# Input transfers, TensorE's order and a few PSUM banks in a fused attention kernel

## The chip, the cores and the metric

The kernel runs on one core of one Trainium2 chip. A core has five engines with instruction queues of their own: TensorE (PE in the profile; PEld is its weight load), VectorE (DVE), ScalarE (ACT), GpSimd (POOL) and SyncE (SP), which here only issues DMAs. Engines meet through semaphores. The metric is device time in microseconds of one execution; lower is better. A page of the profiler and a trace of one profiled execution tell where the time goes.

## The reference, cut to what matters

Three stages, all float32. The input `x` has four samples of 128 channels and 64 x 64 positions (4096 tokens each).

```python
# layer 0: group norm, then attention over the positions of one sample, residual
e1 = prelu(w1 @ xn + b1)           # 64 x 4096, queries
e2 = prelu(w2 @ xn + b2)           # 64 x 4096, keys
asm = prelu(wa @ xn + ba)          # 128 x 4096, values
score = softmax(einsum('nci,ncj->nij', e1, e2), axis=2)
out = einsum('nij,ncj->nci', score, asm)
# layer 1: layer norm over channels, causal running softmax in 8 heads, residual
kv = silu(einsum('btd,ed->bte', x, W_kv)).reshape(b, t, 8, 128, 2)
s = einsum('hd,bthd->bth', q_proj, k)
m_A = cummax(s, axis=1); e = exp(s - m_A)
output = (cumsum(e[..., None] * v, axis=1) / cumsum(e, axis=1)[..., None]).mean(axis=2)
# ffn: 64 experts choose tokens by a gate; two dense layers with gelu; scattered back
```

Layer 0 carries most of the arithmetic: 4 x 4096 x 4096 scores and as many weights for the values.

## The kernel before, in words

**Layer 0.** A sample's queries are cut into 8 blocks (`NBLK`) of 512 (`BLK`), its keys into 16 steps of two chunks of 128. The main loop runs over (sample `b`, query block `qb`, step `p`). In each step `probs` (L563 to L575) has TensorE make two scores tiles (L567), has ACT take their exponential (L571) and DVE add it to an accumulator (L574); `weigh` (L582 to L594) has TensorE multiply the exponentials by the values into two PSUM banks (L592). The exponentials are made one step ahead: `probs(n + 1)` is recorded before `weigh(n)`.

**Preparation of a sample.** `preparation(b)` returns pieces that the loop records one at a time. The statistics are eight `bn_stats` over 512 columns each (L442), their aggregation (L445), and group means by two small matmuls against the constant matrix `gavg` (L449 to L461). Then for each block `k`: `normal(k)` (L468 to L474) writes `xn` on DVE, out of a pool of two buffers; `project(k)` (L488 to L516) multiplies it by the weights of queries and keys (L495), takes the bias on ACT into `y` (L501), forms the prelu (`prelu`, L476 to L486: `z`, the relu of `y`, and their sum `ee`), and sends `ee` to the buffers `e1` and `e2` by DMA; `value(k)` (L520 to L542) multiplies `xn` by the value weights in four matmuls (L525), adds the bias on DVE into `ya` (L537), and forms the prelu likewise into `am`. For sample 0 both write one PSUM tile of two banks, `whole`: projections bank 0, values bank 1.

**Sample 0** has nothing before it to hide its preparation. Its `x` comes in four transfers of 1024 columns, issued in turn by SP and ACT (`load_x`, L387 to L392), followed on ACT's queue by the small weights. `gavg` is built by POOL and DVE and scaled on DVE (L425). After the statistics the blocks 0 and 1 are projected (`work_off(own, 4)`, L661), then the loop starts. In each even step of the first block of queries two more pieces (`project(k)` and `value(k)`) are worked off, ahead of `probs(n + 1)` of that step (L669 to L673); that ends with block 7 in step 10.

**Who sets the order.** Outside a `manual_schedule` a scheduler orders each engine's instructions as it sees fit, subject to dependencies and to `tc.issue_after`, which puts an instruction behind a named one. Dependencies are tracked by tile. Inside a `manual_schedule` for PE, TensorE's instructions keep the order in which they are written. Before the change layer 0 was left to the scheduler, except for its last step, and layer 1's loop was under `manual_schedule`.

**Layer 1.** The loop (L1111 to L1185) runs over 32 blocks of 512 tokens. For block `n` it makes the keys of block `n + 1`: eight heads, each one matmul of 128x512 (L361) into a PSUM bank out of `ps_kv`, and one Silu on ACT (L362) that frees the bank (`keys`, L357 to L363). In the middle stand `weights` (L876 and on, transposes, ACT copy, masks), `values` (L916, Silu L920), the transposes of a later block's tokens (`turned`, L354), `totals` (L932, followed by additions into `before` on DVE, L942), `score`, `scan` (copies of scores, running maximum L834, subtraction L838, exponential L839, running sum, reciprocal; all but the exponential and two copies on DVE), `spread` (`rb`, the reciprocals spread through memory by DMA), and `outputs` (L952). The pools `ps_o` and `ps_t` have one buffer of two banks each: tile `o` is first written in `outputs(0)`, tile `t` in `totals(0)`. For `n = 0` all of block 1's keys come before `values(0)`; heads 4 to 7 of block 0 were made right before the loop's first scan.

**Tail.** After layer 1's loop come the gate and the experts, whose weights are loaded by DMA.

Of the kernel before, what the change touches and what calls it, by code (L numbers as in the profile page):

```python
# [8 lines left out]
F32 = mybir.dt.float32  # L9
AF = mybir.ActivationFunctionType  # L10
ALU = mybir.AluOpType
AX = mybir.AxisListType
PSUM = bass.MemoryType.PSUM
P = 128
# [4 lines left out]
def conv_attn_hybrid_kernel(  # L19
# [23 lines left out]
    nc = tc.nc  # L43
    B, C, N = x.shape
    R = w1t.shape[1]
    NH = qt.shape[1]
# [4 lines left out]
    BLK = 512  # L51
    NBLK = N // BLK
    CPB = BLK // P
# [26 lines left out]
    t = resid.tile([P, B * NCH, C], F32, tag="t", name="t")  # L80
# [245 lines left out]
    def open_banks(stack, pre=""):  # L326
        pool = opener(stack, pre)
        return pool("l1kv", 3, space=PSUM, side="right"), pool("l1s", space=PSUM, side="right")
# [25 lines left out]
            nc.tensor.transpose(ptr[:, c // 2, :, c % 2, :], xl, ident)  # L354
        return nc.scalar.copy(xt, ptr.rearrange("p q s u j -> p (q s u j)")).ins

    def keys(n, xt, heads, kss, ps, pre=""):  # L357

        for h in heads:
            pk = ps.tile([P, BLK], F32, tag="kv", name=f"{pre}pk_{n}_{h}")  # L360
            nc.tensor.matmul(pk, wks[:, h, :], xt, start=True, stop=True)  # L361
            nc.scalar.activation(kss[h], pk, AF.Silu)  # L362
        return [kss[h] for h in heads]  # L363
# [8 lines left out]
    with ExitStack() as l0:  # L372
# [13 lines left out]

        def load_x(b, queues):  # L387
            xs = one.tile([P, N], F32, tag="x", name=f"x_{b}")
            for q in range(4):
                cols = bass.ts(q, N // 4)  # L390
                queues[q % len(queues)].dma_start(out=xs[:, cols], in_=x[b, :, cols])
            return xs  # L392

        xs_of = {0: load_x(0, (nc.sync, nc.scalar))}
# [18 lines left out]
        bas = load("bas", [P, C], (every, ba.to_broadcast([P, C])))  # L413

        neg = wp.tile([P, 2], F32, tag="neg", name="neg")
# [6 lines left out]

        gavg = wp.tile([P, P], F32, tag="gavg", name="gavg")
        make_block_diagonal(nc, gavg, C // 32)
        nc.vector.tensor_scalar_mul(gavg, gavg, 32.0 / C)  # L425

        queries, keys_of, values_of, sent = {}, {}, {}, []

        def preparation(b):
# [34 lines left out]
            xn_of = {}  # L464

            whole = []

            def normal(k):  # L468
                xn = prep.tile([P, BLK], F32, tag="xn", name=f"xn_{b}_{k}")
# [6 lines left out]
            def prelu(dst, y, z, minus_a, negative):  # L476
                if negative is nc.vector:
                    nc.vector.tensor_scalar(
                        out=z, in0=y, scalar1=-1.0, scalar2=0.0, op0=ALU.mult, op1=ALU.max
                    )  # L480
                else:
                    nc.scalar.activation(z, y, AF.Relu, scale=-1.0)
                nc.scalar.activation(y, y, AF.Relu)
                nc.vector.scalar_tensor_tensor(
                    out=dst, in0=z, scalar=minus_a, in1=y, op0=ALU.mult, op1=ALU.add
                )  # L486

            def project(k):  # L488

                xn = xn_of[k]  # L490
                if b == 0:
                    if not whole:
                        whole.append(ps_x.tile([P, 2, BLK], F32, tag="x", name=f"whole_{b}"))
                    pe = whole[0]
                    nc.tensor.matmul(pe[:, 0, :], w12, xn, start=True, stop=True)  # L495
                else:
                    pe = ps_x.tile([P, 2, BLK], F32, tag="x", name=f"pe_{b}_{k}")
                    for u, h in enumerate(halves):
                        nc.tensor.matmul(pe[:, u, :], w12[h, :], xn[h, :], start=True, stop=True)
                y = prep.tile([P, BLK], F32, tag="y", name=f"y_{b}_{k}")  # L500
                nc.scalar.activation(y, pe[:, 0, :], AF.Identity, bias=b12)  # L501
                if b > 0:
                    nc.vector.tensor_add(y, y, pe[:, 1, :])
                z = prep.tile([P, BLK], F32, tag="z", name=f"z_{b}_{k}")
                ee = prep.tile([P, BLK], F32, tag="ee", name=f"ee_{b}_{k}")
                prelu(ee, y, z, neg[:, 0:1], nc.vector if (b, k) == (0, 0) else nc.scalar)
                e1 = qs_p.tile([P, BLK], F32, tag="e1", name=f"e1_{b}_{k}")
                queries[b, k] = e1

                queues = (nc.sync, nc.scalar) if (b, k) == (0, 0) else (nc.sync, nc.sync)  # L510
                by = ee.rearrange("r (j u p) -> r j u p", u=2, p=P)
                for u, (h, queue) in enumerate(zip(halves, queues)):
                    queue.dma_start(out=e1[h, :], in_=ee[halves[0], :])
                    moved = queue.dma_start(
                        out=e2[h, bass.ts(k, CPB // 2), :], in_=by[halves[1], :, u, :]
                    )  # L516
                if (b, k) != (0, 0):
                    sent.append(moved.ins)

            def value(k):  # L520
                xn = xn_of[k]
                if b == 0:
                    pa = whole[0].rearrange("p u (c d) -> p u c d", c=CPB)[:, 1:]
                    for c in range(CPB):
                        nc.tensor.matmul(  # L525
                            pa[:, 0, c, :], xn[:, bass.ts(c, P)], was, start=True, stop=True
                        )
                else:
                    pa = ps_x.tile([P, 2, CPB, C], F32, tag="x", name=f"pa_{b}_{k}")
                    for c in range(CPB):  # L530
                        for u, h in enumerate(halves):
                            nc.tensor.matmul(
                                pa[:, u, c, :], xn[h, bass.ts(c, P)], was[h, :],
                                start=True, stop=True,
                            )
                y = prep.tile([P, CPB, C], F32, tag="y", name=f"ya_{b}_{k}")
                nc.vector.tensor_tensor(  # L537
                    y, pa[:, 0], bas.unsqueeze(1).to_broadcast([P, CPB, C]), ALU.add
                )
                if b > 0:  # L540
                    nc.vector.tensor_add(y, y, pa[:, 1])
                z = prep.tile([P, CPB, C], F32, tag="z", name=f"za_{b}_{k}")  # L542
                prelu(am[:, bass.ts(k, CPB), :], y, z, neg[:, 1:2], nc.scalar)
# [9 lines left out]
        def work_off(blocks, n):  # L553
            for pre, f in blocks[:n]:
                pre()
                f()
            del blocks[:n]
# [24 lines left out]
        def weigh(b, qb, p, pr):  # L582
            am = values_of[b]
            if p == 0:
                av_of[b, qb] = [
                    ps_av.tile([P, BLK], F32, tag=f"av{u}", name=f"av_{b}_{qb}_{u}")
                    for u in range(2)
                ]
            for u in range(2):
                j = 2 * p + u  # L590
                for av, h in zip(av_of[b, qb], halves):
                    nc.tensor.matmul(  # L592
                        av, am[h, j, :], pr[h, u, :], start=(j == 0), stop=(j == NCH - 1)
                    )  # L594
# [63 lines left out]
        with tc.issue_after(root):  # L658
            nc.scalar.activation(seed[:, 1:2], eps5, AF.Exp)
        own = blocks  # L660
        work_off(own, 4)  # L661
        nxt = probs(*steps[0])
        first_sums(0, 0, nxt)
# [2 lines left out]
        end = l0.enter_context(ExitStack())  # L666
        for n, (b, qb, p) in enumerate(steps):
            pr = nxt
            if own and p % 2 == 0:  # L669
                work_off(own, 2)  # L670
                if not own:
                    with tc.issue_after(sent[-1]):
                        xs_of[1] = load_x(1, (nc.sync,))  # L673
            if n + 1 < len(steps):
                nxt = probs(*steps[n + 1])
            if n + 2 == len(steps):
# [3 lines left out]
                for i in range(2):  # L680
                    last_turned = turned(i, xls[i], xts[i], early_room[1])
            weigh(b, qb, p, pr)

            q0 = 1 if b == 0 else 0
            if (qb, p) == (q0, 0) and b + 1 < B:
# [12 lines left out]
            if (b, qb, p) == (B - 1, 1, 0):  # L698
                l0prep.close()
                early_room.append(open_room(early))  # L700
                xts, xl_place, kss = room_parts(early_room[0])
# [64 lines left out]
    def layer1(pre, ready):  # L766
# [6 lines left out]
        with ExitStack() as kept, ExitStack() as l1:  # L773
# [3 lines left out]
            xts, xl_place, kss = room_parts(room)  # L777
# [9 lines left out]
            if ready:  # L787
                ps_kv, ps_s = early_room[1:]
                l1.push(early_banks.pop_all())
            else:  # L790
                ps_kv, ps_s = open_banks(l1, pre)
            ps_o = pool("l1o", space=PSUM)
            ps_t = pool("l1t", space=PSUM)
# [7 lines left out]
            xt_of = {n: xts[n % 3] for n in range(NB)}  # L801
# [309 lines left out]
            def loop():  # L1111
                if ready:
                    ks = keys(0, xt_of[0], range(NH // 2, NH), kss, ps_kv)
# [6 lines left out]
                for n in range(NB):  # L1120
                    more = n + 1 < NB
                    if more:
                        ks = keys(n + 1, xt_of[n + 1], range(NH // 2), kss, ps_kv, pre)
# [4 lines left out]
                    if n + 2 < NB:  # L1128
                        xls = tokens(n + 2, xl_place)
                    if n == 0:  # L1130
                        ks += keys(n + 1, xt_of[n + 1], range(NH // 2, NH), kss, ps_kv, pre)
                    es, rr, _ = made
                    ems = weights(n, es)
                    if n >= 2:
# [126 lines left out]
            with tc.manual_schedule(engines={mybir.EngineType.PE}):  # L1261
# [130 lines left out]
                for g in range(EG):  # L1392
# [10 lines left out]
                    if ready:  # L1403
                        p, k = g // NBLK, g % NBLK
# [29 lines left out]
                for p in range(B // 2):  # L1434
# [8 lines left out]
                    for k0, OB in ((0, 1), (1, 1), (2, 2), (4, 2), (6, 1), (7, 1)):  # L1443
                        for k in range(k0, k0 + OB):
# [10 lines left out]
                            for z in range(2):  # L1455
                                n = (2 * p + z) * NBLK + k
                                at = t[:, bass.ts(n, CPB), :].rearrange("c i x -> c (i x)")
                                nc.vector.tensor_add(at, at, pss[z])
                        for z in range(2):
                            n = (2 * p + z) * NBLK + k0  # L1460
# [65 lines left out]
```

## Time and profile before

| what | us |
|---|---|
| median of 3 runs | 2394.99 |
| lowest to highest | 2394.41 to 2396.77 |
| the profiled execution | 2395.19 |
| its span | 2393.5 |
| start of the first projection (L495) | 14.39 |
| start of the second projection | 20.07 |
| one step of layer 0 in later blocks | 2.57 |
| last copy of the first block's result (L605) | 88.17 |
| first keys of layer 1 (L361) | 1463.73 |

The mean granted clock of TensorE is 0.996. Times in the trace are counted from the start of the span; the profiled execution's own time has 1.7 us more than its span. A line of the timeline gives the start, the duration of a run of like instructions, the engine, the line of code, the operation, output and inputs with their sizes, the number of instructions, and in brackets the idle time of that engine ahead of it with what ended the wait. One float32 matmul of the program shows as two records (x2).

The last transfers are another stretch of interest: in the last 94 us the DMA engines are busy 0.85 of the time and move 332 GB/s, while TensorE is busy 79 of the 94.

### The profile page before, as it was taken

The numbers are of one execution on the slowest core, as the hardware profiler recorded it, in microseconds if no ns is written. First come the engines' busy times: TensorE is split into PE (matmuls) and PEld (weight loads), VectorE is DVE, ScalarE is ACT, GpSimd is POOL, SyncE is SP. The second block draws the span as 40 slices with busy tenths as digits, with TensorE's granted clock in tenths as the row PEclk, the third lists the DMA queues.
The fourth block names the chain that finished last, engine by engine and source line by source line (L and its number), as shares of the span: only waits on it lengthen the run. The fifth ranks groups of instructions, "written<-read, shape, count | busy, mean of one in ns | idle before, by whom it ended". The sixth has DMA issues, their size and how long they took to land.

```text
span 2393.5 us, 45621 instructions
## 1 busy us (share of the span) xinstructions
PE 2347.4 (98%) x19416; PEld 1556.4 (65%) x19416; DVE 1493.6 (62%) x2594; ACT 1208.1 (50%) x1639; POOL 301.4 (13%) x337
## 2 busy tenths in 40 slices
PE   7999999999999999999999999999999999999887
PEld 3467767677778677778777775555555555655553
DVE  5666666666655666655555556666666677776655
ACT  5454444444443444444443435666666666666541
POOL 0000000000000000000000001343343433333300
PEclk9999999999999999999999999999999999999999
DMA  3200020001110000020000000212112121112388
GB/s 81 75 23 14 23 62 1 12 18 23 49 25 1 12 18 23 14 56 1 1 1 1 1 1 19 55 38 52 41 38 55 38 51 42 38 38 55 118 309 318
DMA packets 61189, 109.93 MB, mean 46 GB/s; under 512 B 10032, under 2 KB 35120, under 8 KB 60976
## 3 DMA queue, kind: packets, MB, share of 16 engines
q1 hardware_dynamic: 57536, 101.22, 14.7%
q10 hardware_dynamic: 3440, 5.70, 0.7%
q8 instruction: 154, 2.52, 0.4%
q14 instruction: 59, 0.48, 0.1%
HBM read 85.40 MB, written 8.91 MB: 39 GB/s over the span
## 4 chain that ended last, share of the span: by engine, by line


## 5 line engine op out<-in xcount | busy, mean ns | idle before, releaser
L592 PE MATMUL av<-pr,am 64*128 64x512 f32 x4096 | 1066.2, 591 | 0.0
L571 ACT ACTIVATE pr<-sc 128x1024 f32<-128x1024 f32 x512 | 523.2, 1022 | 676.5 <-PE sc L567 607.7
L574 DVE TENSOR_TENSOR acc<-acc,pr 128x1024 f32<-128x1024 f32 x480 | 586.7, 1222 | 440.4 <-ACT pr L571 440.3
L592 PEld LDWEIGHTS av<-pr,am 64*128 64x128 f32 x4096 | 637.8, 187 | 260.3 <-issue 46.8
L567 PE MATMUL sc<-e,e 64*128 64x512 f32 x2048 | 629.3, 593 | 0.0
L567 PEld LDWEIGHTS sc<-e,e 64*128 64x128 f32 x2048 | 320.2, 187 | 107.6 <-issue 24.5
L361 PE MATMUL pk<-room,wks 128*128 128x512 f32 x512 | 241.1, 610 | 2.6 <-ACT room L362 2.4
L916 PE MATMUL pv<-wvs,room 128*128 128x512 f32 x512 | 226.4, 595 | 2.3 <-ACT v L920 2.3
L920 ACT ACTIVATE v<-pv 128x512 f32<-128x512 f32 x256 | 152.5, 597 | 69.9 <-PE pv L916 69.9
L362 ACT ACTIVATE room<-pk 128x512 f32<-128x512 f32 x256 | 148.0, 597 | 56.7 <-PE pk L361 56.4
L916 PEld LDWEIGHTS pv<-wvs,room 128*128 128x128 f32 x512 | 97.0, 191 | 121.0 <-issue 113.3
L806 POOL MEMSET ew<- 128x1024 f32 x1 | 1.0, 951 | 1364.4 <-PE av L592 1364.4
L904 DVE TENSOR_TENSOR em<-em,rb 128x1024 f32<-128x1024 f32 x64 | 78.4, 1225 | 151.0 <-DMA rb<-rd 150.9
L361 PEld LDWEIGHTS pk<-room,wks 128*128 128x128 f32 x512 | 90.5, 190 | 109.4 <-issue 80.3
L895 POOL TENSOR_TENSOR em<-et,mask 128x1024 f32<-128x1024 f32 x64 | 122.6, 1935 | 82.2 <-ACT et L882 82.2
L952 PEld LDWEIGHTS po<-v,em 64*64 64x64 f32 x4096 | 113.1, 134 | 29.5 <-DVE before L942 26.7
L96 POOL TENSOR_SCALAR xg<-t,gmv,grs 128x128 f32<-128x128 f32 x120 | 94.8, 802 | 287.3 <-DVE grs L92 199.3
L952 PE MATMUL po<-v,em 64*64 64x128 f32 x4096 | 121.1, 273 | 2.5 <-issue 2.5
L854 DVE RECIPROCAL rr<-rr 128x512 f32<-128x512 f32 x32 | 107.3, 3353 | 1.1
L839 ACT ACT_TABLE_LOAD x24 | 30.8, 1283 | 119.8 <-DVE ss L838 119.8
L942 DVE TENSOR_TENSOR before<-before,pt 128x128 f32<-128x128 f32 x256 | 72.5, 283 | 9.6 <-PE pt L932 3.8
L849 DVE TENSOR_TENSOR_SCAN rr<-ones,state,ss 128x512 f32<-128x512 f32 x28 | 42.0, 1502 | 48.1 <-ACT ss L839 48.1
(199 smaller groups left out, 2025.7 us busy)
## 6 DMA issues: line engine op xcount, KB each, us to landing
rb<-rd SPq DMA_DIRECT2D x128, 256.0 KB
fw<-in_fw_dram SPq DMA_DIRECT2D x40, 512.0 KB
room<-in_fw_dram SPq DMA_DIRECT2D x18, 512.0 KB
t<-in_xtok_dram SPq DMA_DIRECT2D x32, 256.0 KB
e<-ee SPq DMA_DIRECT2D x63, 128.0 KB
x<-in_x_dram SPq DMA_DIRECT2D x14, 512.0 KB
e<-ee SPq DMA_DIRECT2D x63, 64.0 KB
out_dram<-t SPq DMA_DIRECT2D x8, 256.0 KB
```

Source lines behind the costliest of these rows:

```text
L96: i = engine.tensor_scalar(out=dst, in0=t[:, chunk, :], scalar1=mean, scalar2=rs, op0=ALU.subtract, op1=ALU.mult)
L361: nc.tensor.matmul(pk, wks[:, h, :], xt, start=True, stop=True)
L362: nc.scalar.activation(kss[h], pk, AF.Silu)
L567: nc.tensor.matmul(sc[:, u, :], e2[halves[u], p, :], e1[halves[u], :], start=True, stop=True)
L571: nc.scalar.activation(pr, sc, AF.Exp)
L574: added.append(nc.vector.tensor_add(acc, acc, pr).ins)
L592: nc.tensor.matmul(av, am[h, j, :], pr[h, u, :], start=(j == 0), stop=(j == NCH - 1))
L854: inverse = nc.vector.reciprocal(rr, rr).ins
L895: nc.gpsimd.tensor_tensor(em, eq.unsqueeze(2).to_broadcast([P, 2 * NH, H2]), mask.unsqueeze(1).to_broadcast([P, 2 * NH, H2]), ALU.mult,)
L916: nc.tensor.matmul(pv.rearrange("p h d -> p (h d)"), xt[:, bass.ts(2 * q + s, P)], wvs[:, bass.ts(m, BLK)], start=True, stop=True,)
L920: last = nc.scalar.activation(v[:, bass.ts(m, HPB), :], pv, AF.Silu).ins
L952: nc.tensor.matmul(po[s * H2 : (s + 1) * H2, u, q, :], aas[q][half, s, h, :], vs[2 * q + s][half, h, :], start=(q == 0 and h == 0), stop=F ...
```

## The change

1. Sample 0's `x` comes in eight transfers of 512 columns instead of four of 1024, on the same two queues in turn.
2. `gavg` is scaled on POOL instead of DVE.
3. The addition `ya` of sample 0's block 0 is put behind `ee` of the same block on DVE.
4. TensorE keeps the written order from the first projections to the end of the first block of queries, and the pieces of `own` blocks are worked off after `weigh` of the step, no longer before `probs`.
5. In layer 1's first round, heads 4 to 7 of block 1's keys are written to the two banks of tile `o` and the two of tile `t`, instead of banks of `ps_kv`.

```diff
-    def keys(n, xt, heads, kss, ps, pre=""):
+    def keys(n, xt, heads, kss, ps, pre="", banks=None):
 
         for h in heads:
-            pk = ps.tile([P, BLK], F32, tag="kv", name=f"{pre}pk_{n}_{h}")
+            if banks:
+                pk = banks.pop(0)
+            else:
+                pk = ps.tile([P, BLK], F32, tag="kv", name=f"{pre}pk_{n}_{h}")
             nc.tensor.matmul(pk, wks[:, h, :], xt, start=True, stop=True)
             nc.scalar.activation(kss[h], pk, AF.Silu)
...
-            for q in range(4):
-                cols = bass.ts(q, N // 4)
+            m = NBLK if b == 0 else 4
+            for q in range(m):
+                cols = bass.ts(q, N // m)
                 queues[q % len(queues)].dma_start(out=xs[:, cols], in_=x[b, :, cols])
...
-        nc.vector.tensor_scalar_mul(gavg, gavg, 32.0 / C)
+        nc.gpsimd.tensor_scalar_mul(gavg, gavg, 32.0 / C)
...
+            scaled = []
...
-                prelu(ee, y, z, neg[:, 0:1], nc.vector if (b, k) == (0, 0) else nc.scalar)
+                scaled.append(
+                    prelu(ee, y, z, neg[:, 0:1], nc.vector if (b, k) == (0, 0) else nc.scalar)
+                )
...
-                nc.vector.tensor_tensor(
-                    y, pa[:, 0], bas.unsqueeze(1).to_broadcast([P, CPB, C]), ALU.add
-                )
+                with ExitStack() as order:
+                    if (b, k) == (0, 0):
+                        order.enter_context(tc.issue_after(scaled[0]))
+                    nc.vector.tensor_tensor(
+                        y, pa[:, 0], bas.unsqueeze(1).to_broadcast([P, CPB, C]), ALU.add
+                    )
...
         own = blocks
+        written = ExitStack()
+        written.enter_context(tc.manual_schedule(engines={mybir.EngineType.PE}))
         work_off(own, 4)
...
-            if own and p % 2 == 0:
-                work_off(own, 2)
-                if not own:
-                    with tc.issue_after(sent[-1]):
-                        xs_of[1] = load_x(1, (nc.sync,))
+            if (b, qb, p) == (0, 1, 0):
+                written.close()
...
             weigh(b, qb, p, pr)
+            if own and p % 2 == 0:
+                work_off(own, 2)
+                if not own:
+                    with tc.issue_after(sent[-1]):
+                        xs_of[1] = load_x(1, (nc.sync,))
...
                     if n == 0:
-                        ks += keys(n + 1, xt_of[n + 1], range(NH // 2, NH), kss, ps_kv, pre)
+
+                        banks = []
+                        for ps, tag in ((ps_o, "o"), (ps_t, "t")):
+                            free = ps.tile([P, 2, BLK], F32, tag=tag, name=f"{pre}pk_{tag}")
+                            banks += [free[:, u, :] for u in range(2)]
+                        ks += keys(
+                            n + 1, xt_of[n + 1], range(NH // 2, NH), kss, ps_kv, pre, banks
+                        )
```

`prelu` now returns its last instruction, so that `scaled[0]` names it.

## Prediction before the run

> **What bounds the kernel now.** I read the page first: which engine is full, which lines fill it, whether it has gaps.
>
> ```profile
> PE 2347.4 (98%) x19416; PEld 1556.4 (65%) x19416; DVE 1493.6 (62%) x2594; ACT 1208.1 (50%) x1639; POOL 301.4 (13%) x337
> ...
> L592 PE MATMUL av<-pr,am 64*128 64x512 f32 x4096 | 1066.2, 591 | 0.0
> ...
> L361 PE MATMUL pk<-room,wks 128*128 128x512 f32 x512 | 241.1, 610 | 2.6 <-ACT room L362 2.4
> ```
>
> TensorE is busy 98% of the span; the chain of waits on the page is empty. Only what TensorE idles (2393.5 - 2347.4 = 46 us), or does more slowly than it could, can be won. What is lost anywhere before the closing stage stays lost to the end. So I took the timeline in three stretches, those that the change touches. The front, DVE and TensorE:
>
> ```profile
> 8.41 2.47 DVE L442 BATCH_NORM_STATS2 stats<-x 128x6 f32<-128x512 f32 x4 [0.15 <-DMA x<-in_x_dram]
> 10.80 0.21 DVE L425 TENSOR_SCALAR gavg<-gavg 128x128 f32<-128x128 f32 x1
> 10.92 0.37 DVE L445 BATCH_NORM_AGGREGATE mv<-stats 128x2 f32<-128x48 f32 x1
> ...
> 17.21 2.08 PE L525 MATMUL whole<-was,xn 128*128 128x128 f32 x8 [0.78 <-ACT y L501]
> ...
> 19.33 0.69 DVE L537 TENSOR_TENSOR ya<-whole,bas 128x512 f32<-128x512 f32 x1 [1.71 <-PE whole L525]
> 19.93 0.74 DVE L484 SCALAR_TENSOR_TENSOR ee<-z,neg,y 128x512 f32<-128x512 f32 x1
> 20.07 2.08 PE L495 MATMUL whole<-xn,w 128*128 128x512 f32 x2 [0.78 <-DVE ya L537]
> ```
>
> Reader: the last statistics, then `gavg`, then the aggregation run back to back; later the second projection waits for `ya`, the last reader of the one tile `whole`. The value matmuls wait for `y`, which reads the *other* bank of that tile: waits go by tile, not by bank. The first block of queries, one period (43.60 to 52.14, 8.54 us, two steps):
>
> ```profile
> 43.60 1.12 PE L495 MATMUL whole<-xn,w 128*128 128x512 f32 x2
> 44.65 1.12 PE L567 MATMUL sc<-e,e 64*128 64x512 f32 x2
> 45.70 1.16 PE L525 MATMUL whole<-was,xn 128*128 128x128 f32 x8
> 46.79 0.69 PE L567 MATMUL sc<-e,e 64*128 64x512 f32 x1
> ...
> 52.14 1.12 PE L495 MATMUL whole<-xn,w 128*128 128x512 f32 x2
> ```
>
> No idle, but half a score pair is drawn in between projection and value, alone, and the pair's other half comes later. The start of layer 1:
>
> ```profile
> 1468.37 1.28 ACT L362 ACT_TABLE_LOAD   x1
> 1469.66 1.57 ACT L362 ACTIVATE room<-pk 128x512 f32<-128x512 f32 x3
> 1470.31 4.22 PE L361 MATMUL pk<-room,wks 128*128 128x512 f32 x6 [2.02 <-ACT room L362]
> 1475.11 7.03 PE L916 MATMUL pv<-wvs,room 128*128 128x512 f32 x16
> ...
> 1491.01 3.74 PE L361 MATMUL pk<-room,wks 128*128 128x512 f32 x8
> 1492.97 1.57 ACT L362 ACTIVATE room<-pk 128x512 f32<-128x512 f32 x3
> ```
>
> TensorE stands 2.02 us for a bank while ACT loads tables; from 1471.6 to 1475.0 its granted clock is 0.50 (window 1472 to 1474), so six matmuls take 4.22.
>
> **What the Trainium skill says.** "TensorEngine Tiling (Array Packing)", Key Properties: a change of tiling mode drains TensorE. The trace agrees: projections of 128*128 among scores of 64*128 take 1.12 where two halves of 0.43 would do, about 0.2 a change. "TensorE: Matmul & The Clock Gate", Part 1: the clock is halved after a mostly idle window of about 3.4 us, on a free-running grid. Here the half-rate stretch is 3.41 long, after a window that was 0.41 busy; windows of 0.55 and more were not punished.
>
> **The change, part by part.**
>
> *Front.* The eight transfers end when four did: from 2 to 8 us the DMA share was 0.97 at 355 GB/s. But the last arrival is followed by two statistics (0.62 each) instead of four: 2 x 0.62 = 1.24 sooner; `gavg`, 0.13, goes to POOL, idle there. ACT issues two transfers more; its small loads now queue behind x, but its table load, ending 11.6, is needed only at about 12.0. `neg` now stands among the group sums and its `a` lands just in time. So normalisation starts 1.24 to 1.37 sooner. It is then given back: in the built order DVE has z, *xn of the third block*, `ee`, `ya`. That xn needs one of two xn buffers, freed by the first block's value matmuls, which end at 19.3 before, 18.05 after. Then 0.04 for the wait, 0.5 xn, 0.66 `ee`, 0.69 `ya` (each without its overlap): 19.95, against 20.02. In before, `ya` went first. The second projection starts 20.00 instead of 20.07: gain 0.07. The clock is half until 27.8 in either.
>
> *First block.* Now TensorE runs as written: scores(n+1), weigh(n), then projection and value with no work between. A period is two steps of 2.57 (5.14, from steady steps of later blocks), projection to end of `y` with the wait (1.16 + 0.69 + 0.06 = 1.91), value with its mode change 1.09: 8.14. Saved 0.40 a period: the split pair's 0.86 and two mode changes go, a wait for `y` of 0.75 comes, with nothing to cover it. Five periods: 2.0. At the start 0.43 is lost: scores twice (24.89 to 28.2, clock half until 27.8), weigh to 29.9, third projection there, fourth at 38.05, which is 35.48 with the extra step of 2.57 taken off; before 35.05. Sum -1.57, the front's 0.07 in it. Does anything come late? Behind the projection, ACT has y, z, relu, za, relu, exp: value ends 3.0, `ya` 3.74, za and relu (0.63 each) to 5.02, exp (1.02) to 6.04; its weigh is due at 3.0 + 0.86 + 1.71 + 0.86 = 6.43. Margin 0.39. e2's DMA has 2 us.
>
> *Layer 1, second block's keys.* Heads 4 to 7 now get two tiles of two banks each, which nobody reads yet. But the dependency is by tile: in the built program head 5 waits for the Silu of head 4, head 7 for that of head 6. Head 5 used to wait for head 2's Silu. ACT's Silus start at 1469.66 (table load) and take 0.52 each: heads 2, 3, 4 end 1471.23. So head 5 starts 1471.27 instead of 1470.31: +0.96. Head 7 waits for Silu 6: head 6's matmul 0.43 after head 5's, its Silu behind Silu 5, about 0.75 of idle: together **+1.7**. The half-rate window still follows, as the window before it is as idle.
>
> Second, DVE's order in that round changes: all six `before` additions (L942) and em stand ahead of the copies of the next scan. Before, three of these were between. About 0.28 each, with the hop to TensorE: the subtraction ends 8.77 after the second block's transposes instead of 7.66. Its Silus release the banks of keys(2), which in before came exactly in time (1493.57). **+1.1**.
>
> *Sum.* -1.57 + 1.7 + 1.1 = +1.2 on the profiled execution, 2395.19 (span 2393.5 and 1.7 around it): 2396.4. The median lies 0.2 below the profiled execution: **2396.2**. TensorE has no gap over 0.5 us between 1493 and 2246, and the last weights are loaded after the loop, so the shift arrives.
>
> Bounds of what the trace of before doesn't show: the two bank waits 0 to 1.7 (taken 1.7, as waits by tile are seen in `whole`); a second half-rate window, 0 to 1.7, as the 0.75 gap falls into it (taken 0); the DVE order 0 to 1.1 (taken 1.1); the front -1.2 to 0 (taken -0.07).
>
> **Rivals.**
>
> A. *The banks are free as meant.* Heads 4 to 7 run through, the window is kept busy, and the 2.02 wait and half clock go, 3.7. But the next scan then waits: rb of the first block lands at 1482.7 whatever TensorE does, em and the scan come behind it, and keys(2) stands about 2.8. Net -0.85. With -1.57: 2392.8, 2392.6 on the median's scale. For it: the banks were unused. Against: the built waits.
>
> B. *Slower: exp comes late in the first block.* Place: ACT, six periods. The margin is 0.39, over six hops between engines which I took at 0.04 to 0.06. From 0.39 on, each 0.1 costs 0.6. If one accumulation of 1.22 (L574) gets ahead of `ya` in time, each period loses 0.83: 6 x 0.83 = +5.0: 2401.2. For it: the chain through ACT and DVE is long and nothing covers it. Against: in the built order `ya` stands behind the accumulation that should be over by 0.53. It decides (over 0.2%) from a lateness of 1.0.
>
> C. *Everything as meant.* The front keeps 1.24, the first block 1.57, the keys 3.7: -6.5, 2388.7, 2388.5 on the median's scale. Against: each of the two givings-back above would have to be absent.
>
> D. *The order doesn't do what it says*: the built order shows it does; only its price is open.
>
> **How the numbers follow.** The likeliest 0.55, own range 2394.2 to 2398.4 (bank waits half as long, or a second half-rate window and more); A 0.12; B 0.22; C 0.11. About 0.2%, 4.8 us, is what a measurement of this kernel tells from no change: 2390.2 to 2399.8. The likeliest and A lie within: 0.67 same. B is slower, 0.22; C faster, 0.11. The range for 8 in 10 takes in the likeliest, A and most of B: 2391.0 to 2401.5.
>
> **What would show it.** Right: first projection near 13.1, but the second still at 20.0; periods of 8.14 with a wait for `y` of 0.7; block end 86.5; in the keys of block 1 two waits on ACT with heads 5 and 7, the first near 3.0; a wait of about 1 at keys(2). Wrong: the second projection at 18.8; periods of 8.5 and more, or a wait of weigh for exp (B); heads 4 to 7 with no wait (A).

## The result, and the profile after

| | before | after |
|---|---|---|
| median of 20 runs, us | 2396.32 | 2400.03 |
| lowest to highest | 2394.41 to 2398.76 | 2397.74 to 2403.41 |
| the profiled execution, us | 2395.19 | 2401.64 |
| its span | 2393.5 | 2399.9 |

The changed kernel takes 1.0015 times as long as the one before, 95% interval 1.0008 to 1.0022. That is 3.7 us slower, clear of noise but inside the 0.2% that the prediction called no change. (Ratios and intervals here and below are worked out from all runs, so they need not be the quotient of the medians beside them.) The two profiled executions are 6.4 us apart: before's was 1.1 under its median, after's 1.6 over. So the traces overstate the difference by 2.7; what in them is chance is named below.

The page's first line after:

```profile
PE 2346.9 (98%) x19416; PEld 1563.0 (65%) x19416; DVE 1494.8 (62%) x2593; ACT 1208.6 (50%) x1639; POOL 303.6 (13%) x338
```

TensorE's busy time is 0.5 us shorter than before, in a span that is 6.4 us longer. On the page the loss is idle time, but the page adds up stretches of opposite sign. From 14 to 95 us TensorE idles 8.2 us instead of 2.8, although the first block ends only 1.5 later, so its matmuls take less time in all. From 1463 to 1500 us it idles 4.6 instead of 2.0, and there more of its matmuls run at half clock. So each of the prediction's three stretches is read for itself. First the front of after, DVE and TensorE (columns as before: start, duration, engine, line, operation, count, and in brackets the wait):

```profile
7.64 2.72 DVE L446 BATCH_NORM_STATS2 stats<-x 128x6 f32<-128x512 f32 x4 [0.52 <-DMA x<-in_x_dram]
10.39 0.37 DVE L449 BATCH_NORM_AGGREGATE mv<-stats 128x2 f32<-128x48 f32 x1
...
18.86 0.55 DVE L475 TENSOR_SCALAR xn<-x,gst,std 128x512 f32<-128x512 f32 x1 [1.71 <-PE whole L532]
19.32 0.75 DVE L489 SCALAR_TENSOR_TENSOR ee<-z,neg,y 128x512 f32<-128x512 f32 x1
19.98 0.69 DVE L547 TENSOR_TENSOR ya<-whole,bas 128x512 f32<-128x512 f32 x1
...
20.72 2.07 PE L500 MATMUL whole<-xn,w 128*128 128x512 f32 x2 [1.90 <-DVE ya L547]
```

Aggregation starts at 10.39, 0.53 sooner than before's 10.92. Then `xn`, `ee` and `ya` stand in a row, and the second projection waits 1.90 for the last: it starts at 20.72, 0.65 *later* than before.

The first block of queries, TensorE alone:

```profile
39.68 1.12 PE L500 MATMUL whole<-xn,w 128*128 128x512 f32 x2
41.58 1.16 PE L532 MATMUL whole<-was,xn 128*128 128x128 f32 x8 [0.78 <-ACT y L506]
42.67 1.13 PE L577 MATMUL sc<-e,e 64*128 64x512 f32 x4
43.63 1.88 PE L602 MATMUL av<-pr,am 64*128 64x512 f32 x8
45.35 1.02 PE L577 MATMUL sc<-e,e 64*128 64x512 f32 x4
46.21 1.88 PE L602 MATMUL av<-pr,am 64*128 64x512 f32 x8
48.02 1.13 PE L500 MATMUL whole<-xn,w 128*128 128x512 f32 x2
```

One period is 48.02 - 39.68 = 8.34 (before 8.54), with a wait of 0.78 for `y` and none of `weigh` for an exponential.

The start of layer 1, TensorE:

```profile
1468.73 1.02 PE L364 MATMUL pk_o<-room,wks 128*128 128x512 f32 x2
1472.75 1.20 PE L364 MATMUL pk_o<-room,wks 128*128 128x512 f32 x2 [3.00 <-ACT room L365]
1473.74 1.92 PE L364 MATMUL pk_t<-room,wks 128*128 128x512 f32 x2
1476.40 2.08 PE L364 MATMUL pk_t<-room,wks 128*128 128x512 f32 x2 [0.75 <-ACT room L365]
1478.27 1.06 PE L894 MATMUL pe<-ident,es 128*128 128x128 f32 x4
1479.12 7.72 PE L930 MATMUL pv<-wvs,room 128*128 128x512 f32 x16
...
1495.70 2.84 PE L364 MATMUL pk<-room,wks 128*128 128x512 f32 x6
1499.35 1.13 PE L364 MATMUL pk<-room,wks 128*128 128x512 f32 x2 [0.81 <-ACT room L365]
```

Heads 4 to 7 show as `pk_o` and `pk_t`; "keys(2)" below stands for the keys of block 2, here the two lines from 1495.70 on. The second head of each tile waits for the Silu of the first, 3.00 and 0.75. Before there was one wait of 2.02. Matmuls take 1.9 to 2.1 where 1.02 is usual: a table of stretches shows a granted clock of 0.50 (columns: us, PE, PEld, DVE, ACT, POOL busy, then clock, DMA share, GB/s).

```profile
1474.00:1480.00 6.00, 5.25 (x10) 2.02 (x10) 0.98 (x2) 1.97 (x4) 0.36 (x1) 0.50 0.26 69
1481.00:1485.00 4.00, 4.00 (x11) 1.75 (x10) 0.66 (x2) 2.85 (x5) 2.41 (x2) 1.00 0.47 114
```

The records of the granted clock show half rate from 1473.7 to 1480.5, two windows of 3.41; before had one.

The prediction put a wait at keys(2) down to DVE's order; the experiment "Additions held" tests that. In after six additions into `before` stand ahead of the first copy of the scan:

```profile
1489.42 1.16 DVE L918 TENSOR_TENSOR em<-em,rb 128x1024 f32<-128x1024 f32 x1
1490.50 1.89 DVE L956 TENSOR_TENSOR before<-before,pt 128x128 f32<-128x128 f32 x6
1492.30 0.42 DVE L843 COPY ss<-ps 128x256 f32<-128x256 f32 x1
...
1494.67 0.69 DVE L852 TENSOR_TENSOR ss<-ss,mm 128x512 f32<-128x512 f32 x1
```

In before three did:

```profile
1484.72 0.23 DVE L942 TENSOR_TENSOR before<-before,pt 128x128 f32<-128x128 f32 x1
1484.87 1.21 DVE L904 TENSOR_TENSOR em<-em,rb 128x1024 f32<-128x1024 f32 x1
1486.00 0.60 DVE L942 TENSOR_TENSOR before<-before,pt 128x128 f32<-128x128 f32 x2
1486.52 0.42 DVE L829 COPY ss<-ps 128x256 f32<-128x256 f32 x1
...
1488.95 0.69 DVE L838 TENSOR_TENSOR ss<-ss,mm 128x512 f32<-128x512 f32 x1
```

**Where the 6.4 us of the two traces lie.** Differences of the same instruction's start, after minus before: start of block 1's keys +1.46 (all of it from the front and the first block); from there to values(0) +2.55 (13.93 against 11.38); the values at half clock +0.69; keys(2) +1.04; keys(3) +0.32. That is 6.06; the rest comes in the tail. The tail is a source of chance: from the transposes of `weights(1)`, which follow the first half of keys(2), to the end, the six traces with before's layer 1, in which that stretch is the same program, take 898.7 to 901.3 us; before takes 898.9 and after 899.6.

### The profile page after: what moved, and what is told of

Read it like the earlier page. It is cut to its first block, busy times and chain, and to the rows that moved or that the text cites. A ratio compares the mean times of both kernels' runs of the same rounds, so it can differ in the third digit from the quotient of the medians.

```text
span 2399.9 us, 45632 instructions
## 1 busy us (share of the span) xinstructions
PE 2346.9 (98%) x19416; PEld 1563.0 (65%) x19416; DVE 1494.8 (62%) x2593; ACT 1208.6 (50%) x1639; POOL 303.6 (13%) x338
## 4 chain that ended last, share of the span: by engine, by line
## 5 line engine op out<-in xcount | busy, mean ns | idle before, releaser
L602 PE MATMUL av<-pr,am 64*128 64x512 f32 x4096 | 1055.5, 591 | 0.0
L577 PE MATMUL sc<-e,e 64*128 64x512 f32 x2048 | 615.4, 594 | 0.0
L364 PE MATMUL pk<-room,wks 128*128 128x512 f32 x504 | 236.3, 607 | 1.5 <-ACT room L365 1.3
```

The source lines that it names most:

```text
L577: nc.tensor.matmul(sc[:, u, :], e2[halves[u], p, :], e1[halves[u], :], start=True, stop=True)
L602: nc.tensor.matmul(av, am[h, j, :], pr[h, u, :], start=(j == 0), stop=(j == NCH - 1))
```

## The experiments

Three theories stood before the first four runs. 1: the loss is made in layer 1, by waits that go by tile and by DVE's order. 2: it is made in layer 0. 3: it is chance of the clock's windows. Line numbers differ by a few from kernel to kernel.

**Banks alone.** The kernel before with part 5 of the change.

```diff
-                        ks += keys(n + 1, xt_of[n + 1], range(NH // 2, NH), kss, ps_kv, pre)
+                        banks = []
+                        for ps, tag in ((ps_o, "o"), (ps_t, "t")):
+                            free = ps.tile([P, 2, BLK], F32, tag=tag, name=f"{pre}pk_{tag}")
+                            banks += [free[:, u, :] for u in range(2)]
+                        ks += keys(
+                            n + 1, xt_of[n + 1], range(NH // 2, NH), kss, ps_kv, pre, banks
+                        )
```

> The kernel before, with only the keys' banks of layer 1 as in the change. Theory 1 (the loss is made in layer 1, by waits that go by tile and by DVE's order): head 5 waits 3.0 us and head 7 0.75 us for ACT; from the start of block 1's keys to the start of values(0) 13.9 us at the same clock windows (11.4 before); one wait of about 0.8 at keys(2); time 3 to 4 us over before, ratio about 1.0015. Theory 2 (the loss is made in layer 0, by the written order and the front; banks are neutral in the sum): not more than 1 us over before. Theory 3 (the loss is chance of the clock's windows): no part alone shows more than 1 us.

Measured: 2398.54 against 2395.41, ratio 1.0013 (1.0006 to 1.0019). Waits of 3.00 and 0.75 in the keys, 0.80 at keys(2); from block 1's keys to values(0) 14.07. Theory 1 holds: this part alone makes most of the loss, 3.1 us in the medians. Theory 3 falls with that, as the account of the whole loss: by it no part alone was to show more than 1 us.

**The change without the banks.** Parts 1 to 4 alone.

```diff
...
-                        ks += keys(
-                            n + 1, xt_of[n + 1], range(NH // 2, NH), kss, ps_kv, pre, banks
-                        )
+                        ks += keys(n + 1, xt_of[n + 1], range(NH // 2, NH), kss, ps_kv, pre)
```

> The changed kernel with the keys' banks of layer 1 as before; the front and the written order stay. Theory 1: within 1.5 us of before (front and first block cost 0 to 1 together), no wait at keys(2), one wait of 2.0 us in block 1's keys. Theory 2: 3 us and more over before. Theory 3: within 1 us.

Measured: 2395.98 against 2395.41, ratio 1.0003 (0.9995 to 1.0011). One wait of 2.02, none at keys(2). Theory 2 falls: parts 1 to 4 together cost less than the 3 us that it asked for, and what they do cost can't be told from nothing. In this trace no half-rate window follows the wait of 2.02; the stretch to values(0) is 9.69 instead of before's 11.38.

**Banks in turn.** Same two tiles, but the second head goes to the other tile.

```diff
+                        banks = [banks[i] for i in (0, 2, 1, 3)]
                         ks += keys(
```

> The kernel before, with the keys' heads 4 to 7 in the unused banks, but the two tiles taken in turn (first bank of o, first of t, second of o, second of t), so that head 5 follows a head of another tile. Theory 1: head 5 runs straight after head 4; head 6 waits for the Silu of head 4, at about the time at which head 5 waits in the change, but with one matmul less behind it and no second wait of 0.75: values(0) start about 1.2 us sooner than with the banks in the change's order; DVE has before's order and keys(2) wait not at all; time 0 to 1.5 us over before. Theory 2 and 3: no difference to the banks in the change's order.

Measured: 2395.9 against 2395.41, ratio 1.0003 (0.9994 to 1.0011). The timeline of its keys:

```profile
1467.06 1.02 PE L364 MATMUL pk_o<-room,wks 128*128 128x512 f32 x2
1467.92 1.02 PE L364 MATMUL pk_t<-room,wks 128*128 128x512 f32 x2
1471.08 1.95 PE L364 MATMUL pk_o<-room,wks 128*128 128x512 f32 x2 [2.14 <-ACT room L365]
1472.83 1.91 PE L364 MATMUL pk_t<-room,wks 128*128 128x512 f32 x2
```

Head 5 runs straight behind head 4 because it stands in another tile; head 6, again in tile `o`, waits for the Silu of head 4. The banks are the same four and as unused as in the change; only which head shares a tile with which is different. So the wait is the tile's, not the bank's. DVE has before's order, and keys(2) does not wait. From block 1's keys to values(0) it is 11.52, 2.55 less than with the banks in the change's order: more than the 1.2 expected, as only one half-rate window follows and not two. The time, 0.5 us over before, is in the range expected.

**Additions held.** Banks as in the change, but DVE is given before's order of the additions in the first round: three ahead of the scan's copies, the rest put behind its steps (`release` is called behind each copy, the running maximum and the subtraction).

```diff
+            held = []
+
+            def release(after, count=1):
+                for _ in range(min(count, len(held))):
+                    with tc.issue_after(after):
+                        held.pop(0)()
...
-                for x in range(GRP):
+                def add(x):
...
+                now = 3 if n == 0 else GRP
+                for x in range(now):
+                    add(x)
+                held.extend(lambda x=x: add(x) for x in range(now, GRP))
```

> The kernel before with the keys' banks as in the change, and with the additions into before of the first round put on DVE as they stood in the kernel before: three ahead of the next scan's copies, the others among and behind its steps. Theory (DVE's order is what makes the wait at keys(2)): the wait of 0.8 there is 0.1 or nothing, while the waits of 3.0 and 0.75 in block 1's keys stay; time about 1 us less than with the change's banks alone (within its interval). Rival (the wait at keys(2) comes from the later em or from the banks themselves): it stays 0.8.

Measured: 2399.38 against 2396.3, ratio 1.001 (1.0001 to 1.0018). The second wait in block 1's keys, and keys(2) in one piece, where after has 2.84 and then a wait of 0.81:

```profile
1475.41 1.13 PE L364 MATMUL pk_t<-room,wks 128*128 128x512 f32 x2 [0.74 <-ACT room L365]
...
1492.70 3.86 PE L364 MATMUL pk<-room,wks 128*128 128x512 f32 x8
```

The waits in block 1's keys are as in the change (3.00 and 0.74). The one at keys(2) is gone, though the second `em` ends 3.90 after the block's transposes here as in after, and though the banks are those of the change. The subtraction of the scan ends 7.77 after the block's transposes (1491.45 - 1483.68); in after 8.68, in before 7.66. So the order on DVE makes the wait. In the time the 1 us can't be told from the banks alone: the intervals overlap.

**Own tiles.** Before, with heads 4 to 7 in four tiles of one bank, given back before tiles `o` and `t` are made.

```diff
+            free, late = ExitStack(), {}
+            ps_free = opener(free, pre)("l1free", 4, space=PSUM)
...
-                        ks += keys(n + 1, xt_of[n + 1], range(NH // 2, NH), kss, ps_kv, pre)
+                        ks += keys(n + 1, xt_of[n + 1], range(NH // 2, NH), kss, ps_free, pre)
+                        free.close()
+                        for tag in ("o", "t"):
+                            late[tag] = opener(l1, pre)("l1" + tag, space=PSUM)
```

> The kernel before, with heads 4 to 7 of block 1's keys in four tiles of one bank each, which are given back before the two tiles of two banks are made. Theory (waits go by tile): none of heads 4 to 7 waits, from the start of block 1's keys to values(0) 7.4 us instead of 9.7 (without half clock) to 11.4 (with it), no half-rate window there. Then the scan of block 1 is late, as rb of the first block lands no sooner: a wait of 2 to 3.5 us at keys(2); so time 0 to 2 us less than before. Rival (what is won stays won): no wait at keys(2), 2.3 to 4 us less than before.

Measured: 2395.92 against 2396.12, ratio 0.9997 (0.9989 to 1.0005). Its timeline:

```profile
1463.70 7.13 PE L361 MATMUL pk<-room,wks 128*128 128x512 f32 x16
1470.67 0.60 PE L880 MATMUL pe<-ident,es 128*128 128x128 f32 x4
...
1482.41 0.87 PE L952 MATMUL po<-v,em 64*64 64x128 f32 x21
1484.16 3.27 PE L952 MATMUL po<-v,em 64*64 64x128 f32 x107 [0.87 <-issue]
...
1492.00 1.13 PE L361 MATMUL pk<-room,wks 128*128 128x512 f32 x2 [0.78 <-ACT room L362]
```

All eight heads run in 7.13 without a wait. The gain is given back at once: 0.87 in `outputs(0)` and 0.78 at keys(2), together 1.65, where 2 to 3.5 was expected, all of it at keys(2). The line does not name what ends the 0.87. By the code it is the second half of `em`, which waits for `rb`, and the times fit: `rb` is sent no sooner than before (1475.74, before 1475.78), and the first matmul that needs that half starts 0.41 after it has ended (0.39 in the last experiment, where the same wait comes at another time). The trace has the idle time 43 records ahead of that matmul, so this is a fit and no proof.

The stretch in one table, from the start of block 1's keys to the transposes of `weights(1)`, which follow the first half of keys(2):

| kernel | us | half-rate windows |
|---|---|---|
| before | 30.85 | 1 |
| change without banks, and every other kernel with before's keys | 29.16 or 29.17 | 0 |
| after, and banks alone | 35.12 and 35.11 | 2 |
| additions held | 32.87 | 1 |
| banks in turn | 30.98 | 1 |
| own tiles | 29.26 | 0 |

Own tiles win nothing against before's keys at full clock (29.26 against 29.16). What they can win is a half-rate window's 1.69 (30.85 - 29.16), when there would have been one.

**Eight transfers alone.** Before, with parts 1 and 2.

```diff
-            for q in range(4):
-                cols = bass.ts(q, N // 4)
+            m = NBLK if b == 0 else 4
+            for q in range(m):
+                cols = bass.ts(q, N // m)
...
-        nc.vector.tensor_scalar_mul(gavg, gavg, 32.0 / C)
+        nc.gpsimd.tensor_scalar_mul(gavg, gavg, 32.0 / C)
```

> The kernel before, with eight transfers for the first sample and gavg scaled on POOL, nothing else. As the trace after shows aggregation 0.53 sooner and not 1.24: aggregation near 10.4, first projection near 13.9, and, with before's order on DVE (ya ahead of the third xn), the second projection near 19.6, 0.5 sooner than before. Rival: the third xn gets ahead of ya here too, second projection at 20.7. Time: 0.5 us less than before, or with the rival 0.7 more; either is inside the spread of the runs.

Measured: 2395.34 against 2395.41, ratio 1.0 (0.9991 to 1.0008). Aggregation at 9.86, the second projection at 19.21, 0.86 sooner than before: better than expected, and the third `xn` stays behind `ya`. The aggregation of a kernel with eight transfers starts at 9.86 to 10.39 (six traces, mean 10.14), with four at 10.83 to 11.10 (six, mean 10.97): 0.83 sooner, not 1.24, and it varies by 0.5.

**Without the order of `ya`.** The change without banks and without part 3.

```diff
-                    if (b, k) == (0, 0):
-                        order.enter_context(tc.issue_after(scaled[0]))
```

> The changed kernel with the keys' banks as before and without putting ya behind ee; eight transfers, gavg on POOL and the written order stay. DVE then has ya ahead of the third xn. Theory: the second projection starts near 19.3 and not 20.6, its wait for DVE is 0.78 and not 1.90; as the clock is half until about 28, half of the 1.4 arrives: first block 0.7 shorter than with the order of the change at the same clock windows; periods of the first block stay 8.34. Rival (the third xn goes ahead for another reason): 20.6 as before. Time within 1 us of before.

Measured: 2394.67 against 2396.12, ratio 0.9991 (0.9983 to 0.9999). The second projection starts at 19.46 with a wait of 0.78, against 20.64 and 1.90 with part 3 in it. So part 3 lets the third `xn` ahead of `ya`, which costs 1.2 at that place. Of the 0.7 expected at the block's end 0.3 is seen at most: in the last column of the table below it is 78.50 here and 78.23 with part 3, but in the 78.50 there is a wait of 0.59 for the first exponential that the other doesn't have. The time was to be within 1 us of before; it is 1.45 less in the medians, at the edge of what can be told from nothing.

**Written order alone.** Before with part 4.

```diff
+        written.enter_context(tc.manual_schedule(engines={mybir.EngineType.PE}))
...
-            if own and p % 2 == 0:
-                work_off(own, 2)
...
             weigh(b, qb, p, pr)
+            if own and p % 2 == 0:
+                work_off(own, 2)
```

> The kernel before with TensorE's written order in the first block and nothing else of the change. Theory (from the trace after): second projection at 20.1 as before, periods 8.34 with a wait for y of 0.78, five of them 1.0 less than before's, 0.4 to 1.0 more at the start, where scores and a weigh come before the third projection and the clock is half: exp of the block's end within 0.6 of before's once half the difference of the clock's change is taken off; time within 1 us. Rival, the prediction's own sum: 1.5 us less.

Measured: 2397.38 against 2396.3, ratio 1.0001 (0.9993 to 1.0009). Periods of 8.34. For the end of the first block I take the first exponential of the next block that waits 1.74 us (at 91.79 in before). The time at which the clock goes from half to full, which differs from trace to trace, is in it with about half its amount, and the last column takes that half off:

| kernel | second projection | clock full from | block's end | end less half of the clock's time |
|---|---|---|---|---|
| before | 20.07 | 27.79 | 91.79 | 77.90 |
| four others with before's layer 0 | 19.99 to 20.25 | 27.40 to 28.78 | 91.58 to 92.35 | 77.85 to 77.98 |
| eight transfers alone | 19.21 | 27.84 | 91.38 | 77.46 |
| written order alone | 20.19 | 26.58 | 92.02 | 78.73 |
| the same, eight transfers (no order of `ya`) | 19.46 | 25.53 | 91.26 | 78.50 |
| the change without banks | 20.64 | 28.87 | 92.66 | 78.23 |
| after | 20.72 | 29.84 | 93.27 | 78.35 |
| scores between | 19.21 | 27.09 | 87.29 | 73.74 |

The five traces with before's layer 0 agree to 0.13 in the last column and spread over 0.77 in the one before it, so taking off half is about right. (In the two rows with the earliest clock TensorE waits 0.44 and 0.59 for the first exponential, so an early clock does not pay in full there and the last column is that much too high.) Taking those waits off or leaving them, written order costs 0.4 to 1.0 against before's own schedule (78.73 against 77.90, 78.50 against 77.46); the prediction had 1.5 gained. This run's 0.83 is over the 0.6 expected unless the wait of 0.44 is taken off. After lies 0.45 over before, and 1.02 of the 1.48 by which its first block ends later is the clock's chance.

**Scores between.** As the run without the order of `ya`, with the next scores written between projection and value, to cover the wait for `y`.

```diff
                 nxt = probs(*steps[n + 1])
+            if own and p % 2 == 1:
+                work_off(own, 1)
...
             if own and p % 2 == 0:
-                work_off(own, 2)
+                work_off(own, 1)
```

> As the last one, with TensorE's written order changed in the first block: the next scores stand between projection and value, so that they cover the wait for y. Theory (the wait of 0.78 is what the written order pays): no wait between projection and value, periods near 7.7 instead of 8.34 (1.05 projection, 1.05 scores with two changes of mode, 1.09 value, two weighs of 1.8, one score pair of 0.86), five of them 3.2 us less; time 2 to 4 us less than before, ratio 0.9985 to 0.999. Rival (the exponentials come late on ACT): periods stay over 8.2 with waits of weigh for ACT.

Measured: 2391.85 against 2396.12, ratio 0.9982 (0.9974 to 0.999). One period:

```profile
44.63 1.12 PE L497 MATMUL whole<-xn,w 128*128 128x512 f32 x2
45.69 1.13 PE L573 MATMUL sc<-e,e 64*128 64x512 f32 x4
46.74 1.16 PE L529 MATMUL whole<-was,xn 128*128 128x128 f32 x8
47.83 1.99 PE L598 MATMUL av<-pr,am 64*128 64x512 f32 x8
49.65 1.02 PE L573 MATMUL sc<-e,e 64*128 64x512 f32 x4
50.51 1.88 PE L598 MATMUL av<-pr,am 64*128 64x512 f32 x8
52.33 1.13 PE L497 MATMUL whole<-xn,w 128*128 128x512 f32 x2
```

No bracket, no wait: 7.70 a period, as expected, and the block ends 4.16 sooner than before in the last column of the table, 0.44 of it from the eight transfers. In the medians it is 4.3 us less than before, a little more than the 2 to 4 expected. The wait for `y`, bare in the written order, is what kept that order from paying.

**All together.** Scores between, and own tiles for the keys; both diffs stand above.

> The two last ones together: eight transfers, gavg on POOL, scores between projection and value, and four tiles of one bank for the keys. Theory: the sum of both, 3 to 5 us less than before, ratio near 0.998. If the wait at keys(2) takes all that the keys win: 2 to 4 us less.

Measured: 2391.6 against 2396.12, ratio 0.9977 (0.9967 to 0.9986). The waits of own tiles come again (0.76 in `outputs`, 0.88 at keys(2)), so it can't be told from the scores between alone. Both beat the kernel before, and by their ratios the changed one, beside which they were not run.

## Why the prediction held, and which terms were off

The forecast was no change beyond 0.2%, at +1.2 us; measured +3.7. The direction was right, the change is within 0.2%, and 2400.03 lies in the wide range. The narrow range of the likeliest account, 2394.2 to 2398.4, was missed, taken as a time or as a difference (-0.8 to +3.4). Part of the rest is luck. From the three runs of before that the prediction had (median 2394.99) it put the limit of no change at 2399.8, and 2400.03 lies over that; with twenty runs before's median rose to 2396.32. And the wide range reached so far up because of rival B, which didn't come. What the prediction got right is the mechanism at the start of layer 1; what it got wrong, the first block and the second half-rate window, it had both times put too favourably. Term by term:

- *Bank waits, +1.7.* Right to the hundredths: head 5 was to wait 2.98 and waited 3.00; head 7 was to wait 0.75 and waited 0.75. That the tile decides was read from `whole` in the trace of before, and banks in turn shows it.
- *DVE's order, +1.1.* Right: +1.04 in keys(2), the subtraction 8.68 after the transposes where 8.77 was worked out. Additions held shows the cause.
- *A second half-rate window, taken as nothing, bounded at 1.7.* It came, in after and in banks alone, and in the way that the prediction had named: the gap of 0.75 falls into the first half-rate window, which is then busy 0.78 of its length and is followed by another. In additions held the same gap falls almost wholly behind that window (busy 0.97), and in before there is no gap (1.00); there the clock goes back to full. So it was wrong to take it as nothing; by the table of the stretch it was 1.5 in after (35.12 - 30.85, less 1.73 of bank waits and 1.04 in keys(2)). The first window is not certain either: with the wait of 2.02 one trace of six had one, with 3.00 all three had one or two.
- *Front, -0.07.* The step that gives the gain back was right (`xn`, `ee`, `ya`, in this order), but the gain to be given back was 0.53 and not 1.24: the prediction took the last landing as unchanged, and with transfers of 256 KB DVE's last wait for `x` ended at 9.07, where before's ended at 8.41. So the second projection came at 20.72 and not 20.00. With the clock at half until later, about half of the 0.65 arrives.
- *First block, -1.57.* This is the term that failed in sign: +0.45 in after at like clock. The period was put at 8.14 from two steps of 2.57; in the written order two places take 0.10 more, one where scores follow values (0.96 to the next instruction against 0.86), one where the projection follows `weigh` (1.81 against 1.71). At both the lines show the form of the matmuls change between 128*128 and 64*128; that this change is what costs the 0.10 is argued, not shown. (The prediction read about 0.2 for one change out of before, where a projection among scores takes 1.05 to the next instruction; against 0.86 that is 0.19 for two.) So a period saves 0.20, not 0.40. The start costs more too: the fourth projection, with the extra step taken off, was to be 0.43 late and was 2.06 late, of which 1.02 is the clock and 0.33 the front. From there to the block's end 0.58 is won, not 2.0.
- *Rival A, banks free as meant, -0.85.* Own tiles is that rival made real. Its later wait was put at 2.8 in one place and is 1.65 in two. It wins nothing at full clock, and its time can't be told from before's: as the rival said, what is won ahead of `rb` is for the most part waited for behind it.
- *Rival B, late exponentials.* Not seen: no `weigh` waits for ACT in the periods of after. The margin of 0.39 held.
- *A reading.* The "six matmuls" that take 4.22 are six records, and so three matmuls. No term rests on it.

The terms as measured: 1.7 + 1.0 + 0.45 is 3.2, and a second window adds up to 1.7 where it comes; measured 3.7, of which the banks alone make 3.1. How often the other executions had one or two windows isn't known: of each of them only the mean granted clock of the whole span is on record, to three places, and a window is 0.0007 of it. But the clock's chance doesn't make the loss. At the mean that is recorded most often, 0.996, nine executions of after average 2398.65 and 56 of before, run with the experiments, 2395.47: 3.2 apart.

## What to carry to other kernels

Storage that nobody uses is not storage without waits: if two writers share a tile, the second waits for the first's reader, so give each its own tile or put the writers of one tile as far apart as possible. An order written by hand removes the scheduler's detours, such as the split score pair, and with them the work that filled a wait; look for the wait that it lays bare, and write something into it (here a wait of 0.78 a period stood between a change worth nothing and 4.3 us). Before filling a stall at the start of a loop, ask what the next round waits for.

## What the runs showed of the hardware that was not expected

The time at which TensorE goes to full clock after the start differed between traces of the same front by 1.4 us (27.40 to 28.78 for five traces), and over all kernels from 25.53 to 29.84. Each microsecond of it moved the first block's end by about half a microsecond. So what is won in a stretch at half clock pays half: eight transfers alone brought the second projection 0.86 forward and the block's end 0.44.

The same wait of 2.02 us at the start of layer 1 was followed by a window at half clock in one trace of six and by none in five, and that window costs 1.69. "TensorE: Matmul & The Clock Gate" of the Trainium skill, Part 1, has the clock halved after an idle window of about 3.4 us, on a free-running grid. The traces agree with the grid: in all five that have a half-rate window there, it begins 423 windows, 1443.84 us, after the clock went full at the start (in before 27.79 and 1471.63, in after 29.84 and 1473.67), whenever the wait itself began. They show more than the page on how idle such a window must be. In the stretch of 3.41 that ends where the half rate begins, TensorE was busy 0.41 of the time in before, 0.37 in banks in turn, and 0.27, 0.23 and 0.12 in the three kernels that wait 3.00. In the five traces in which the same 2.02 was not followed by half rate, the wait lies across a border of the grid, and the emptier stretch was busy 0.44 to 0.53. So the chance is in where the wait falls. An estimate from these numbers: to take 2.0 us out of one stretch of 3.41, a wait of 2.02 has about 0.4 of the possible places, one of 3.00 about 0.7. The limit between the two is not sharp: in the tail, stretches busy 0.44 to 0.50 were followed by either rate.

The difference of 2.7 us by which the two traces overstate the medians is of the size of what differs by chance between traces: 1.02 in the first block, up to 1.7 for a half-rate window, 2.5 between the shortest and the longest tail. That these make it up is argued, not shown.
